# Where the narrow products of the next group's x stand in layer 1 of a four-layer kernel

## The chip, the core and the metric

The kernel runs on one core of one Trainium2 chip. The metric is the device time of one execution in microseconds. The engines are named as in the profile: PE is TensorE's matmuls and PEld its weight loads, DVE is VectorE, ACT is ScalarE, POOL is GpSimd and SP is SyncE, which here only issues copies.

## The reference

x has 64 sequences of 32 rows of 512 numbers, so 2048 rows. Four layers follow one another, each of the form x = x + ffn(cond(x)). The change lies in the second of them, layer 1. Its cond part is a gated network with a low-rank addition chosen for each sequence:

```python
def lora_add(base, inp, A, B):          # A[n]: 16 x inputs, B[n]: outputs x 16, n chosen by the sequence
    t = einsum('bri,bni->bnr', A[ids], inp)
    return base + einsum('bor,bnr->bno', B[ids], t) * 0.5
gate = lora_add(x @ W_gate.T, x, A_gate, B_gate)      # 512 -> 1376
up   = lora_add(x @ W_up.T,   x, A_up,   B_up)        # 512 -> 1376
act  = silu(gate) * up
down = lora_add(act @ W_down.T, act, A_down, B_down)  # 1376 -> 512
```

Its ffn part takes the result through a 512 x 512 product with a bias and a gated mixture of eight low-rank updates; its output is added to x. Layer 0 is a mixture over squared ReLU features, layer 2 attention over a cache of keys and values, and layer 3 again products with low-rank updates. All numbers are float32.

## The kernel before

Layer 1 is `layer1`, from L323. It works on groups of two tiles of 128 rows, so a group is 256 rows, or eight sequences, and there are eight groups. The products of a group are held transposed: features stand on the partitions and the 256 rows in the free dimension.

A product with a sequence's own A is narrow. For two sequences at a time the 16 rows of A for each stand side by side, so that a product has 32 columns of weights and 64 moving columns; four such products, one for each pair of sequences, fill four strips of 32 output partitions in one PSUM tile. `low` (L416) does this for x: two matrices (gate and up), four slices of 128 inputs and four pairs of sequences, 32 products into `low_ps`. `low_down` (L428) does it for the activations: eleven slices of features and four pairs, 44 products into `low_d_ps`. Each is followed by `masked` (L407), one VectorE instruction that multiplies the result with a mask, so that each sequence keeps its own 16 numbers, and writes `low_x` or `low_d`. Those are the inputs of one more full-width product each with the gathered B rows: `features` (L439) uses `low_x` with Bg1 and Bu1, and `down` (L455) uses `low_d` with Bd1.

A product of float32 appears in the profile as two matmuls and two weight loads, so one call of `product` makes two records on PE and two on PEld.

The order of TensorE's work is written out by hand: `on_pe` (L76) makes each matmul follow the one written before it. The loop from L539 goes over the groups. `new` is the group in work, `old` the one before, whose ffn part (`choose`, `base`, `turn`, `out`) is spread between the features of `new`, and `then` the one after. Eleven calls of `features` make the 1376 features (the last has 96). In between, `then` gets its gathered rows and its A copies (`load_updates`, L378), its x (`load_x`), the transposes of it (`x`, L398) and a rearranged copy of A for x (`firsts("x")`, L387, on VectorE, tile `first_x`). At the end stand the down products: `new.down(range(NFC - 1), False)` makes 4 x 10 products over the first ten feature slices into `pz`, and `new.down((NFC - 1,), True)` makes, for each of four output slices, one product for the last feature slice and one with Bd1, and then copies `pz` to `zT`. This place, from the first down product to the first gate product of the next group, is called a turn; the group after it exists in seven of the eight cases.

The other engines' lists are ordered by a scheduler. In the program before, VectorE's list has, behind the last features of a group, the masking of `low_d`, the copy `first_down` for the next group, the masking of `low_x`, the copy `first_x` for the group after that (each group has one place for `first_x`, and the copy waits for eight A copies), and the copy to `zT`. SyncE's queue issues the A copies, x and the blocks of weights for `sum_up` (L274) in a chain; `sum_up` prepares sums of layer 2's weights on GpSimd beside the features, and the gathered Bg1, Bu1 and Bd1 rows are issued on GpSimd behind the last sum.

Of the kernel before, what the change touches and what calls it, by code (L numbers as in the profile page):

```python
# [322 lines left out]
def layer1(c, kp, x_in, x_out, sums):  # L323

    tc, nc, a = c.tc, c.nc, c.a
    G = 2
    N = G * P  # L330
# [5 lines left out]
    with ExitStack() as ctx:  # L336
# [28 lines left out]
        def product(out, lhsT, rhs, start, stop):  # L365
            c.on_pe(nc.tensor.matmul(out, lhsT, rhs, start=start, stop=stop))  # L366

        class Group:
# [70 lines left out]
            def features(self, f):  # L439

                if f == 0:
                    self.actT = gp.tile([P, NFC, N], F32, name="actT")
                o, w = FC[f]
                acc = ps.tile([P, 2, N], F32, tag="acc", bufs=4, name="gate_up")
                for u, (wt, n) in enumerate(((wg, "Bg1"), (wu, "Bu1"))):
                    for k in range(KC):
                        product(acc[:w, u, :], wt[:, k, o:o + w], self.xT[:, k, :],
                                u == 0 and k == 0, False)
                    product(acc[:w, u, :], self.B[n][:, o:o + w], self.low_x[:, u, :], False, u == 1)
                sg = tp.tile([P, N], F32, name="sg")  # L450
                nc.scalar.activation(sg[:w], acc[:w, 0, :], AF.Sigmoid)  # L451
                nc.vector.tensor_tensor(sg[:w], sg[:w], acc[:w, 0, :], ALU.mult)  # L452
                nc.vector.tensor_tensor(self.actT[:w, f, :], sg[:w], acc[:w, 1, :], ALU.mult)
# [85 lines left out]
        for g, new in enumerate(groups):  # L539
            old = groups[g - 1] if g else None  # L540
            then = groups[g + 1] if g + 1 < len(groups) else None
            parts = [f for _ in range(5) for f in next(to_sum)]

            def features(f):
                new.features(f)
                if f < len(parts):
                    parts[f]()

            features(0)
            if old:  # L550
                old.choose(0)
            features(1)
            if old:
                old.choose(1)
            features(2)
            new.firsts("down")
            if then:
                then.load_updates()
            features(3)
            if old:  # L560
                old.turn(0)
                old.base(0)
                old.out(0)
            features(4)
            if old:
                old.turn(1)
                old.base(1)
                old.out(1)
            if then:
                then.load_x()  # L570
            features(5)
            features(6)
            features(7)
            if then:
                then.x(0)
            features(8)
            if then:
                then.x(1)
            features(9)
            if then:  # L580
                then.firsts("x")
            features(10)
            new.down(range(NFC - 1), False)
            new.low_down()
            if then:
                then.low()
            new.down((NFC - 1,), True)
        for f in (new.choose, new.base, new.turn, new.out):
            for t in range(G):
# [897 lines left out]
def emit(tc, a, layers=(0, 1, 2)):  # L1487
    with ExitStack() as ctx:
# [11 lines left out]
        for n in layers:  # L1500
            out = rows("out") if n == layers[-1] else scratch(f"x{n}")
            if n == 0:
                layer0(c, x, out)
            if n != 0 and n == next(m for m in layers if m):
                kp = ctx.enter_context(tc.tile_pool(name="known", bufs=1))
                last = Tail(c)
                last.numbers(kp)
                known = Known(c, kp)
                sums = {}
                for h in range(HALVES):  # L1510
                    sums["in", h] = dram.tile([P, GB, 4, KC // 2, D], F32, name=f"in_sums{h}")
                    sums["out", h] = dram.tile([P, HQP // 2, 4, D // 2], F32, name=f"out_sums{h}")
            if n == 1:
                layer1(c, kp, x, out, sums)
            elif n == 2:
                y_part, y = scratch("y_part"), scratch("y")
                attention(c, known, x, y_part, y, sums, last.between(x, y, out))
            x = out
# [86 lines left out]
```

## Time and profile before

| what | us |
|---|---|
| median of 3 plain runs | 3589.3 |
| lowest and highest | 3585.83, 3597.19 |
| the profiled execution, whole | 3603.64 |
| its span, first to last instruction | 3601.9 |
| TensorE matmul busy (98% of the span) | 3526.7 |
| TensorE weight loads busy (73%) | 2634.1 |
| VectorE busy (60%) | 2154.5 |
| GpSimd busy (44%) | 1598.8 |
| layer 1, about | 388 to 1073 |

Where the text speaks of a moment it is counted from the start of the span. A line of the chain of waits, or of the timeline, has the start, the duration, and then what ran: engine, line, output and inputs by the program's names, and how many of them. "issue" is time in which an engine waited for nothing that the profile shows. The granted clock is the share of TensorE's full clock that it was given.

### The profile page before, as it was taken

How to read it: one execution, taken by the hardware profiler on the slowest of the kernel's cores; microseconds unless marked ns; L12 is line 12 of the kernel's file. 1: busy time of each engine (PE TensorE's matmuls, PEld its weight loads, DVE VectorE, ACT ScalarE, POOL GpSimd, SP SyncE). 2: the span in 40 equal slices, each digit the busy share in tenths (PEclk: the TensorE clock that was granted, in tenths of full speed). 3: DMA queues.
4: the chain of work that ended last, by engine and by line, in shares of the span. 5: the costliest groups of instructions: out<-in, count | busy, mean ns of one | idle time of the engine just before them, and what ended most of it. 6: DMA issues, size and time to landing. Idle time of an engine off the chain costs nothing.

```text
span 3601.9 us, 61460 instructions
## 1 busy us (share of the span) xinstructions
PE 3526.7 (98%) x19328; PEld 2634.1 (73%) x19328; DVE 2154.5 (60%) x5268; ACT 1301.2 (36%) x3110; POOL 1598.8 (44%) x1607
## 2 busy tenths in 40 slices
PE   8999999999998999999999999999999999999999
PEld 3444788877875777787787777877877778777755
DVE  5443222222227777778778677787787777877433
ACT  1111111111113545444454454444544544444311
POOL 0112332222207546456455464564564655644232
PEclk9999999999999999999999999999999999999999
DMA  5003543333226777888877878788878788877731
GB/s 210 27 26 136 174 135 125 103 103 105 101 72 213 249 243 249 256 248 257 255 248 253 258 247 255 249 257 258 255 254 263 245 264 253 256 253 223 217 94 63
DMA packets 610340, 715.99 MB, mean 199 GB/s; under 512 B 61826, under 2 KB 469378, under 8 KB 610018
## 3 DMA queue, kind: packets, MB, share of 16 engines
q1 hardware_dynamic: 557538, 539.01, 48.2%
q0 software_dynamic: 50176, 168.86, 13.4%
q10 hardware_dynamic: 2304, 4.20, 0.3%
q8 instruction: 157, 2.57, 0.3%
q14 instruction: 165, 1.35, 0.1%
HBM read 669.88 MB, written 41.94 MB: 198 GB/s over the span
## 4 chain that ended last, share of the span: by engine, by line
PE 84%; DVE 8%; DMA 3%; issue 2%; POOL 1%; ACT 1%; SPq 1%; DVEq 0%; another core or an unknown queue 0%; ACTq 0%; POOLq 0%
PE po L712 12%; PE gate_up L366 11%; PE py L712 11%; PE sc L993 10%; PE pq L712 7%; PE prT_ps L707 5%; PE pkv L712 5%; PE pz L366 5%; PE po L1371 3%; PE ph L126 3%; PE pd L251 3%; PE po L366 2%; PE qkT_ps L707 1%; PE py L206 1%; DVE pr L1005 1%
## 5 line engine op out<-in xcount | busy, mean ns | idle before, releaser
L738 POOL DMA_INDIRECT vt<-in_v_rows,v_rows x512 | 510.9, 998 | 313.3 <-PE po L712 189.8
L1000 ACT ACTIVATE pr<-pr,low 128x544 f32<-128x544 f32 x512 | 383.3, 749 | 688.1 <-DVE low L998 556.3
L993 PE MATMUL sc<-kt,qT 128*128 128x288 f32 (+1 forms) x2048 | 557.2, 395 | 15.5 <-DVE low L998 12.6
L993 PEld LDWEIGHTS sc<-kt,qT 128*128 128x128 f32 x2048 | 386.2, 191 | 232.2 <-issue 129.3
L712 PE MATMUL po<-prT,vt 128*128 128x128 f32 x4096 | 546.9, 277 | 4.8 <-ACT prT L1011 3.1
L712 PEld LDWEIGHTS po<-prT,vt 128*128 128x128 f32 x4096 | 522.3, 192 | 39.6 <-ACT prT L1011 20.7
L998 DVE CUSTOM_DVE_ANT_0 pr<-sc,mask 128x544 f32<-128x544 f32 x512 | 368.4, 719 | 142.9 <-PE sc L993 119.2
L786 POOL TENSOR_TENSOR projected<-projected,swapped 128x512 f32<-128x512 f32 x160 | 208.3, 1302 | 313.5 <-DVE projected L785 284.5
L1005 DVE TENSOR_SCALAR pr<-pr,low 128x512 f32<-128x512 f32 x512 | 318.4, 622 | 12.6
L1011 ACT COPY prT<-prT_ps 128x512 f32<-128x512 f32 x512 | 294.0, 574 | 75.3 <-PE sc L993 30.8
L707 PE MATMUL prT_ps<-ident,pr 128*128 128x128 f32 x2048 | 312.5, 275 | 1.8 <-DVE pr L1005 1.7
L707 PEld LDWEIGHTS prT_ps<-ident,pr 128*128 128x128 f32 x2048 | 238.5, 142 | 10.4 <-issue 2.1
L712 PE MATMUL py<-wo,oT 128*128 128x256 f32 x1024 | 241.8, 379 | 0.0
L712 PE MATMUL pq<-wp,x_sums 128*128 128x512 f32 x512 | 240.2, 593 | 0.0
L1002 DVE RECIPROCAL low<-low 128x1 f32<-128x1 f32 x512 | 82.1, 160 | 229.7 <-ACT pr L1000 195.3
L712 PEld LDWEIGHTS py<-wo,oT 128*128 128x128 f32 x1024 | 186.5, 190 | 21.1
L1003 ACT ACTIVATE own_pr<-pr,low 128x32 f32<-128x32 f32 x512 | 164.8, 322 | 93.6 <-DVE low L1002 68.5
L452 DVE TENSOR_TENSOR sg<-sg,gate_up 128x256 f32<-128x256 f32 (+1 forms) x88 | 37.0, 421 | 269.3 <-ACT sg L451 265.9
L130 POOL TENSOR_TENSOR rs<-rs,minus_half 128x4 f32<-128x4 f32 x160 | 180.6, 1129 | 23.3 <-DVE low L1002 15.7
L712 PE MATMUL py<-wo,o_sum 128*128 128x256 f32 x768 | 182.9, 382 | 2.3 <-DVE o_sum L929 2.3
L712 PE MATMUL pq<-wp,xT 128*128 128x512 f32 x384 | 182.2, 597 | 0.2 <-issue 0.2
L745 DVE COPY own_vt<-v 32x128 f32<-32x128 f32 x512 | 164.1, 320 | 22.8 <-issue 4.0
(242 smaller groups left out, 5856.2 us busy)
## 6 DMA issues: line engine op xcount, KB each, us to landing
kt<-in_kT SPq DMA_DIRECT2D x2048, 64.0 KB
wp<-in_sums SPq DMA_DIRECT2D x192, 512.0 KB
wo<-out_sums SPq DMA_DIRECT2D x128, 512.0 KB
wp<-in_WqT SPq DMA_DIRECT2D x96, 512.0 KB
wo<-in_WoT SPq DMA_DIRECT2D x96, 512.0 KB
wp<-in_WkT SPq DMA_DIRECT2D x32, 512.0 KB
xt<-x SPq DMA_DIRECT2D x48, 256.0 KB
in_sums<-sums POOLq DMA_DIRECT2D x24, 512.0 KB, 5.1
```

The costliest lines, as they stand in the source:

```text
L130: self.nc.gpsimd.tensor_tensor(t, t, self.minus_half[:, :n], ALU.pow)
L366: c.on_pe(nc.tensor.matmul(out, lhsT, rhs, start=start, stop=stop))
L707: c.on_pe(nc.tensor.transpose(pt[:, m, :], piece, c.ident))
L712: c.on_pe(nc.tensor.matmul(out, lhsT, rhs, start=first and i == 0, stop=last and i == len(pairs) - 1))
L738: nc.gpsimd.indirect_dma_start(out=vts[b % 2][:, n, :], out_offset=None, in_=a["v_rows"], in_offset=bass.IndirectOffsetOnAxis(ap=rows[h][: ...
L786: nc.gpsimd.tensor_tensor(src, src, tmp, ALU.add)
L993: c.on_pe(nc.tensor.matmul(sc[:, lo + n * PSIZE:lo + m * PSIZE].rearrange("p (n k) -> p n k", k=PSIZE), q, kt[:, n:m, g, :], start=True, s ...
L998: nc.vector.tensor_tensor_reduce(pr[:, :NK], sc[:, lo:lo + NK], masks[h, b], -SCALE, 3.0e38, ALU.add, ALU.min, low[:, 0:1])
L1000: nc.scalar.activation(pr[:, :NK], pr[:, :NK], AF.Exp, bias=low[:, 0:1], scale=-1.0, accum_out=low[:, 1:2])
L1003: nc.scalar.activation(own_prs[b % 2][:, g * S:(g + 1) * S], pr[:, L:NK], AF.Copy, scale=low[:, 2:3])
L1005: nc.vector.tensor_scalar(pr[:, :L], pr[:, :L], low[:, 2:3], None, ALU.mult)
L1011: last_prT.append(nc.scalar.copy(prT, pt).ins)
```

## The change

In each turn with a group after it, `then.low()` moves from behind `new.low_down()` to ahead of the first down products. Nothing is added or left out. In the built program, VectorE's list changes with it: the masking of `low_x` and the copy `first_x` for the group after next come ahead of the masking of `low_d` and the copy `first_down`. The lists of ScalarE, GpSimd and SyncE are the same as before.

```diff
             features(10)
+            if then:
+                then.low()
             new.down(range(NFC - 1), False)
             new.low_down()
-            if then:
-                then.low()
             new.down((NFC - 1,), True)
```

## The prediction

> **What bounds the kernel now.** I read the page first: TensorE is busy 3526.7 us of the 3601.9 us span, so time is saved only where TensorE itself stands still or runs slowly. The queue list of the same page holds a second fact that matters here: a queue of kind "instruction", q8.
>
> ```profile
> PE 3526.7 (98%) x19328; PEld 2634.1 (73%) x19328; DVE 2154.5 (60%) x5268; ACT 1301.2 (36%) x3110; POOL 1598.8 (44%) x1607
> ...
> q8 instruction: 157, 2.57, 0.3%
> ```
>
> 2.57 MB in 157 packets is 16.4 KB each. TensorE has 2 x 19328 = 38,656 records (a weight load and a matmul count one each), and 38,656 / 157 = 246 records a packet. I take q8 to be TensorE's own code.
>
> Next, the chain of waits, cut to layer 1. The change acts at a place that comes seven times, where a group has a group after it; I number these turns 1 to 7 and measure each from the first down product to the first gate product of the next group. Turns 6 and 7:
>
> ```profile
> 867.34 17.27 PE pz L366 x80
> 884.61 1.37 PE low_d_ps L366 x88
> 885.97 0.89 PE low_ps L366 x62
> 886.86 4.07 issue
> 890.93 0.42 PE low_ps L366 x2
> 891.35 6.28 PE pz L366 x16
> ...
> 956.67 17.27 PE pz L366 x80
> 973.94 1.37 PE low_d_ps L366 x88
> 975.31 0.89 PE low_ps L366 x64
> 976.20 3.66 PE pz L366 x16
> ```
>
> Turn 7 is the clean one: 17.27 + 1.37 + 0.89 + 3.66 = 23.2 us. In turn 6 TensorE stops for 4.07 us two records before the end of the narrow products, with no semaphore to blame ("issue"), and then needs 6.28 us instead of 3.66 for the same 16 products. The stretches of all seven turns, with busy times by engine (PE, PEld, DVE, ACT, POOL), then granted clock, DMA share and GB/s:
>
> ```profile
> 442.32:467.69 25.37, 24.23 (x250) 20.73 (x249) 4.07 (x6) 0.97 (x2) 14.24 (x19) 1.00 0.64 206
> 526.74:550.99 24.25, 23.35 (x249) 20.31 (x249) 3.98 (x6) 0.97 (x2) 8.94 (x12) 1.00 0.51 168
> 610.03:633.23 23.20, 23.20 (x250) 20.32 (x249) 3.98 (x6) 0.97 (x2) 8.73 (x12) 1.00 0.49 165
> 692.27:719.50 27.23, 25.03 (x250) 21.50 (x249) 3.98 (x6) 0.97 (x2) 9.20 (x12) 0.94 0.46 150
> 778.55:808.29 29.74, 26.43 (x249) 22.44 (x249) 3.98 (x6) 0.97 (x2) 9.39 (x13) 0.89 0.46 150
> 867.34:897.63 30.29, 26.22 (x249) 22.36 (x249) 4.08 (x6) 0.97 (x2) 8.97 (x12) 0.89 0.43 143
> 956.67:979.87 23.20, 23.20 (x250) 20.32 (x249) 3.38 (x5) 0.97 (x2) 11.02 (x17) 1.00 0.40 138
> ```
>
> Against 23.20 the excess is 2.17, 1.05, 0, 4.03, 6.54, 7.09 and 0: **20.9 us** in all. Turns 2, 4, 5 and 6 hold 0.90 + 2.20 + 3.31 + 4.07 = 10.5 us of "issue" in one piece each; the other 8.2 us of their 18.7 are the slow clock after it (granted clock 0.50 in 715.8 to 719.1, 801.1 to 807.8 and 889.9 to 896.5). Turn 1 stutters in four short pieces.
>
> Why does TensorE stop? The DMA view, cut to turn 6, shows no q8 packet from 884.6 to 888.4, while POOL's queue q0 moves 0.86 MB at a DMA share of 62%; the q8 packet comes at about 888.5, and TensorE goes on at 890.9. In turn 7 the same kind of packet passes in 973.0 to 974.5 with no other traffic, and nothing stops. Over the first three microseconds or so of the narrow products the DMA share was 0.93, 0.73, 0.77 and 0.62 in the four stalled turns, and 0.15 and 0.03 in the clean ones. So I read it thus: 88 + 64 narrow products are 304 records in 2.26 us, more than one packet of code, and the next packet stands behind the gathered Bg and Bu rows that POOL issued a few microseconds earlier (880.71 and 882.03 in turn 6).
>
> **The change part by part.** Nothing is added or taken away. TensorE's order is written out by hand, so its list follows the source: in each turn the 32 products of low (64 records of each kind) go ahead of the 40 down products, and low_down's 44 stand alone behind them. ScalarE's, POOL's and SyncE's lists stay as they are, every DMA with them. On VectorE two instructions go ahead of low_d: the masking of low_x (0.68 us) and the copy of first_x for the group after next (0.68 us).
>
> (1) The code supply. The narrow run of 304 records becomes 128 (0.89 us) and 176 (1.37 us), with 160 wide records, 17.27 us, between. A packet of 246 records that holds all of low_down holds 70 wide records, 35 matmuls at 0.216 us (17.27 / 80): 7.6 + 1.4 = 9.0 us of work. The slowest packet, turn 6, took 6.3 us (884.61 to 890.93), counted from the start of the narrow run. Counted so, it now comes in time with 2.7 us to spare. Value: from 0 (the stall only moves) to +20.9 us. I count turns 2 to 6 in full (18.7 us) and half of turn 1 (1.1 us), whose stutter begins before its packet and has another look: **+19.8 us**.
>
> Here a rule speaks against the gain. The Trainium skill, "Runtime: NRT & Kernel Launch", section "Instruction fetch mechanics", says that crossing a 16 KiB boundary of code is mostly hidden, because instructions are dispatched more slowly than the store of code is refilled. By the rule the 20.9 us aren't code and term (1) is nothing; the change would then cost only term (2), 3590.7 us. The row decides: 304 records in 2.26 us are 7.4 ns each, and the stops end 1.4 us after a q8 packet has run. The page's packet of 256 instructions agrees with the 246 above.
>
> (2) Lost cover for low_d. Before, low's 0.89 us stood between low_down and the products with Bd1, which need VectorE's masked low_d (0.42 us). Now one down product of 0.43 us is all. The trace has this arrangement already, in the last group, which has no group after it:
>
> ```profile
> 1055.23 1.44 PE L366 MATMUL low_d_ps<-actT,first_down 128*32 128x64 f32 x88
> 1056.60 0.70 PE L366 MATMUL pz<-actT,down1T 96*128 96x256 f32 x2
> 1056.73 0.42 DVE L410 TENSOR_TENSOR low_d<-low_d_ps,own 128x256 f32<-128x256 f32 x1 [17.39 <-PE low_d_ps L366]
> 1057.21 0.70 PE L366 MATMUL pz<-low_d,Bd 128*128 128x256 f32 x2
> ```
>
> There the chain gives 3.86 us to the 16 products instead of 3.66: 0.2 us, times seven: **-1.4 us**. Queued behind the waiting product are the other six products of this tail and the next group's gate products, so all of it is on the path. If VectorE were late, each microsecond would count in full.
>
> (3) low comes earlier. It needs xT: ScalarE's second copy follows the second transpose (517.66 in turn 2), a whole pair of features, 8.63 us, before low would start. It needs first_x, copied a turn earlier, and for the first turn at 425.03, 17 us ahead. Both are hidden, 0; if xT came late the wait would stand in front of the down products one for one.
>
> (4) low_x is ready some 18 us sooner. Its reader, the Bg product at 552.34 in turn 2, found it done (547.30 + 0.68) anyway: 0.
>
> (5) VectorE's queue. The copy of first_x waits for eight A copies, and low_d, the next first_down and the copy of zT now queue behind it. The A copies were issued at 522.95 to 526.63 in turn 2, and the hardware queue's traffic was over by about 532; low_down would end at 526.7 + 0.89 + 17.27 + 1.37 = 546.2, so 14 us are left. Turns 3 to 6 issue A at the same place. Turn 1 is the tight one: A issued until about 455, traffic over by 459.5, low_down over at 461.8. Hidden, 0, with 2.3 us of cover there.
>
> Sum: 19.8 - 1.4 = 18.4 us. The profiled execution took 3603.6 us (1.7 us around the span), so its like would take 3585.2. The median of the plain runs, 3589.3, is 14.3 us lower; the order of the code is the same in both, so I carry the difference over whole: 3589.3 - 18.4 = **3571 us**, -0.5%.
>
> **The rivals.** (a) The plain runs stall less than the profiled one, since the wait for code depends on DMA traffic in that execution. For it: turns 3 and 7 don't stall at all. Against it: four of seven do, and the copies in their way are the kernel's own. With half of the gain, 9.9 - 1.4 = 8.5: 3581 us.
>
> (b) The change doesn't do what it says: TensorE still runs dry, now in the single runs or just behind them, since the same records pass. For it: the 6.3 us may have begun earlier than I count, and 9.0 us isn't far above. Against it: the last group's low_down, alone among wide products, ran with no stop, and turn 2 lost only 0.9 us at the highest DMA share. Then 20.9 is kept and 1.4 lost: 3591 us.
>
> (c) Slower: VectorE's wait for A. If A lands after low_down's end, low_d is held back by the copy of first_x, and TensorE with it. It decides once A lands over 19.5 us after a turn begins; to be slower than before with the stalls gone it takes (18.4 + 10.8) / 7 = 4.2 us more in each turn. Now A lands at about 5 us in turn 2 and 17 us in turn 1. It could come later if POOL's sums, which SyncE's queue waits for ahead of A, fall behind the faster groups. With 5 us in each turn: 3589.3 - 18.4 + 35 = 3606 us.
>
> **How the numbers follow.** A plain comparison of this kernel tells about 0.3% (10.8 us) from no change. Likeliest case 0.70, own range 3564 to 3578; (a) 0.14; (b) 0.10; (c) 0.06. Half of (a) may lie over the bound, as its gain runs from 4 to 13 us: faster 0.70 + 0.09 = 0.79, same 0.05 + 0.10 = 0.15, slower 0.06. The range: up to 3586 it takes in most of (a), down to 3562 a gain of 27 us, some 6 more than the profile shows, for plain runs that stall longer. Left out are (b), (c) and a little more.
>
> **What would show it.** Right: seven turns near 23.4 us from the end of the features to the next gate product (0.89 + 17.27 + 1.37 + 3.86), no "issue" over 0.5 us beside low_ps or low_d_ps, granted clock 1.00 from 400 to 1060. Wrong: idle time of one to four microseconds with a q8 packet in it behind low_d_ps; VectorE's low_d released by an A copy; the Bd product later than 0.3 us behind low_d; or the same stops elsewhere in the layers behind, whose code comes at other moments beside their DMAs.

## The result

The changed kernel took 3575.2 us, the median of six runs (3569.5 to 3582.5), against 3592.8 us for the kernel before in six runs beside them and earlier (3585.8 to 3597.3). The ratio is 0.9963, with a 95% interval of 0.9950 to 0.9977: faster by 0.37%, which is 13 us by the ratio and 17.6 us by the medians. Run twice more, each time beside the kernel before on the same chip, it came to 0.9970 (0.9956 to 0.9984) and 0.9960 (0.9947 to 0.9974). The forecast was 3571 us in a range of 3562 to 3586, so time and direction were right.

These are the seven turns of the changed kernel, each from its first narrow product of x to the first gate product of the next group, with the same columns as the seven rows shown of before (busy time of PE, PEld, DVE, ACT and POOL, then granted clock, DMA share, GB/s):

```profile
443.18:466.89 23.71, 23.71 (x249) 20.48 (x250) 4.48 (x6) 0.97 (x2) 13.84 (x18) 1.00 0.60 193
525.93:549.64 23.71, 23.71 (x250) 20.47 (x250) 4.66 (x6) 0.97 (x2) 9.27 (x12) 1.00 0.49 168
608.69:632.40 23.71, 23.71 (x249) 20.48 (x250) 4.08 (x6) 0.97 (x2) 8.83 (x12) 1.00 0.49 163
691.44:715.15 23.71, 23.71 (x250) 20.48 (x250) 4.08 (x6) 0.97 (x2) 9.18 (x12) 1.00 0.55 169
774.20:797.90 23.70, 23.70 (x249) 20.47 (x250) 4.08 (x6) 0.97 (x2) 10.07 (x13) 1.00 0.61 194
856.95:880.66 23.71, 23.71 (x250) 20.48 (x250) 4.51 (x6) 0.97 (x2) 9.32 (x13) 1.00 0.56 184
939.71:963.42 23.71, 23.71 (x249) 20.48 (x250) 3.38 (x5) 0.97 (x2) 10.12 (x15) 1.00 0.45 152
```

Every turn is the same, PE is busy through each of them, and the clock is full. The sum is 166.0 us; before it was 183.3, so the turns gave 17.3 us. The profiled executions differ by more, 3603.6 - 3582.5 = 21.2 us; the other 3.9 us lie outside the turns. The chain of waits shows what one turn is made of, here turn 6, the one that had stopped for 4.07 us:

```profile
856.95 1.03 PE low_ps L367 x64
857.98 17.46 PE pz L367 x80
875.45 1.37 PE low_d_ps L367 x88
876.82 3.85 PE pz L367 x16
```

No "issue" is left. But low costs 1.03 us where it had cost 0.89, the down products 17.46 instead of 17.27, and the tail 3.85 instead of 3.66: each turn is 0.51 us longer than the clean turn of before (23.20 us). The first two differences, 0.33 us, were not in the forecast.

### The profile page after: what moved, and what is told of

It is laid out like the page before. It is cut to its first block, busy times and chain, and to the rows that moved or that the text cites. A ratio compares the mean times of both kernels' runs of the same rounds, so it can differ in the third digit from the quotient of the medians.

```text
span 3580.7 us, 61453 instructions
## 1 busy us (share of the span) xinstructions
PE 3519.5 (98%) x19328; PEld 2630.8 (73%) x19328; DVE 2156.9 (60%) x5268; ACT 1297.6 (36%) x3110; POOL 1598.2 (45%) x1607
## 3 DMA queue, kind: packets, MB, share of 16 engines
q14 instruction: 165, 1.35, 0.1%
## 4 chain that ended last, share of the span: by engine, by line
PE 88%; DVE 4%; DMA 4%; issue 1%; POOL 1%; ACT 1%; SPq 0%; DVEq 0%; ACTq 0%; POOLq 0%
PE po L713 13%; PE sc L994 11%; PE py L713 11%; PE gate_up L367 11%; PE pq L713 8%; PE prT_ps L708 6%; PE pkv L713 5%; PE pz L367 5%; PE po L1372 3%; PE ph L126 3%; PE pd L251 3%; PE po L367 2%; PE qkT_ps L708 2%; DMA wp<-in_sums 1%; PE py L206 1%
## 5 line engine op out<-in xcount | busy, mean ns | idle before, releaser
L708 PEld LDWEIGHTS prT_ps<-ident,pr 128*128 128x128 f32 x2048 | 238.0, 142 | 10.9 <-issue 2.7
L288 POOL TENSOR_TENSOR sums<-blocks 128x256 f32<-128x256 f32 x40 | 28.9, 723 | 330.6 <-DMA blocks<-in_WoT 109.7
```

Source lines behind the costliest of these rows:

```text
L708: c.on_pe(nc.tensor.transpose(pt[:, m, :], piece, c.ident))
```

## The experiments

The question was what stops TensorE, and why the change ends it. The code theory says that a packet of code comes too late when it is used up in one narrow run while the next waits in the DMA queues. Its main rival was that a long narrow run stops by itself, wherever the packets end; the question beside it was how much POOL's gathers have to do with it.

**Where the stops stand.** The traces answer part of this without an edit. TensorE's list in the kernel before has 40,373 instructions: 38,656 matmuls and weight loads, 1,714 that handle semaphores, and three more. q8 brought 157 packets of 16,384 bytes; at 256 instructions each these are 40,192, so a packet holds 256, and the forecast's 246 had left out the semaphores. Counted in the order in which they ran, these are the instructions ahead of each long stop:

| profile | turns | instructions ahead of the stop |
|---|---|---|
| kernel before | 2, 4, 5, 6 | 4801, 6849, 7873, 8897 |
| kernel before, once more (below) | 2, 3, 4, 5, 6 | 4801, 5825, 6849, 7873, 8897 |
| no gathers (below) | 5, 6, 7 | 7873, 8897, 9921 |

Divided by 256, every one of these twelve leaves 193. So these stops are whole packets apart, as packet ends are, wherever in the turn they fall. The four of turn 1 aren't (211, 221, 100 and 111 are left). In the kernel before, a group takes 1030 instructions, six more than four packets, so the packet end moves six back from one turn to the next: from the tail in turn 2 to the last products of low in turn 6.

**The packet ends moved, the order kept.** Ahead of layer 1's first narrow products:

```diff
+        spare = ps.tile([P, P], F32, tag="lo", bufs=2, name="spare")
+        for n in range(32):
+            product(spare[:, :64], c.ident, c.ident[:, :64], n == 0, n == 31)
         groups[0].low()
```

> The kernel before, with 32 small products of the identity (128x64 moving, two matmuls and two loads each, 128 records) put once ahead of layer 1's first narrow products. Their result is read by nobody. The order of the turns stays: 304 narrow records in one run. Code theory: all later packet ends move by 128 records against the turns. Where TensorE ran dry after 300 to 322 records of the narrow run, packet ends now lie at about 172 to 194, and the packet that begins there holds some 120 narrow, 32 tail and 100 feature records, over 14 us of work, so it is refilled in time: turns 2, 4, 5 and 6 fall to about 23.2 us, excess over all turns under 4 us instead of 20.9, and a plain time 12 to 18 us under the kernel before (the added products cost 2 us). Rival, narrow run as such: 304 narrow records beside POOL's gathers stop TensorE wherever the packets end; excess stays at 15 to 25 us, plain time within 5 us of before.

The ratio to the kernel before was 0.9986 (0.9979 to 0.9992), with a median of 3593.1 against 3596.4 us. Turn 6 in its chain of waits:

```profile
863.54 17.27 PE pz L366 x80
880.80 1.37 PE low_d_ps L366 x88
882.17 0.89 PE low_ps L366 x64
883.07 3.67 PE pz L366 x16
```

TensorE's order is that of before, 304 narrow records in one run, and there is no stop, in this turn or in any other: the sum of these rows is 23.2 us, and the periods from group to group are 82.24 us, all six. Only the place of the packet ends has changed. The rival falls. The plain time gained 3 to 5 us and not 12 to 18, for the most part because the added products cost some 10 us and not 2. They ran at half clock (0.51 granted from 387.8 to 400.55 us), which by itself explains no more than a factor of two:

```profile
387.80 12.75 PE L366 MATMUL spare<-ident 128*128 128x64 f32 x60
```

Layer 1's first narrow product came at 400.5 us instead of 390.2. In the profiles layer 1 still ended 10.9 us sooner than in the first profile of before (1062.2 against 1073.1).

**Half that shift.** The same with `range(16)`, 64 records.

> The kernel before with 16 small products of the identity, 64 records, ahead of layer 1's first narrow products; it runs dry, if at all, 64 records earlier in the narrow run, about 236 to 258 records into it. Two readings of when a packet of code is asked for. If it is asked for when the packet before it begins to run, that is 2 us ahead of the narrow run and behind GpSimd's gathers (issued 2 to 4 us ahead of it): stops in turns 5 and 6 as long as before or 0.5 us longer, 4 to 5 us. If it is asked for some 40 records sooner, because TensorE's queue is filled ahead of its work, that is 6 us ahead of the narrow run and ahead of the gathers: no stop over 0.6 us in turns 4 to 6, group periods of 82.2 to 82.5 us. Rival, narrow run as such: stops of 1 to 4 us as in the kernel before.

One run, 3573.8 us, and again no stop of 0.2 us or more in any turn, with periods of 82.24 us and one of 82.43. So of the two readings the second holds, and the traces bear out its 40 records: in the first profile of before, seven of layer 1's 31 packets began exactly 41 instructions ahead of the end of the packet in work, and none more than 45 ahead. In the kernel before this point falls on the start of the narrow run, behind POOL's gathers; 64 records sooner it falls among the wide products, ahead of them. Turn 6 of this run: q8 from 869.5 to 871.0 us (packets, MB, share), then Bg:

```profile
q8 instruction: 1, 0.02, 3.9%
```

```profile
874.53 1.00 POOL L360 DMA_INDIRECT Bg<-in_Bg,rows  x1 [0.30 <-issue]
```

The packet began at 869.88 us, 4.7 us ahead of Bg's issue. In turns 2, 4 and 5 it was ahead as well, by 0.2 to 1.8 us; in the same four turns of the kernel before it began 6.4 to 7.8 us behind Bg's issue.

**No gathers.**

```diff
-                self.B = {n: gather(n, g) for n in ("Bg1", "Bu1", "Bd1")}
+                self.B = ({n: gather(n, g) for n in ("Bg1", "Bu1", "Bd1")} if g < 2
+                          else groups[g - 2].B)
```

> The kernel before, but groups from the third on use the gathered Bg1, Bu1 and Bd1 rows of the group two before them, so 18 of 24 gathers are left out and the layer computes with the wrong rows there. TensorE's list is unchanged. Code theory with the queue: the packet of code no longer stands behind the gathers. Turns 2, 4, 5 and 6 lose most of their stop and their slow clock, excess under 5 us in all, plain time 12 to 18 us under the kernel before. Rival, the packet is late by itself: the narrow run takes 2.26 us and any packet takes longer, so each of these turns keeps a stop of 1 to 2 us, excess 8 to 15 us. Rival, narrow run as such: unchanged, 15 to 25 us.

The ratio was 0.9971 (0.9960 to 0.9982), 3587.5 against 3596.4 us: 9 us less, somewhat under what was expected. Turns 2 to 4 have no stop; in turns 5, 6 and 7 a small one grows. Turns 6 and 7 in the chain of waits:

```profile
871.58 0.90 PE low_ps L366 x64
872.48 0.41 PE pz L366
872.89 0.64 issue
873.52 3.41 PE pz L366 x15
...
954.62 0.89 PE low_ps L366 x63
955.50 1.43 issue
956.93 0.22 PE low_ps L366
957.15 3.66 PE pz L366 x16
```

Turn 6 has lost most of its stop (0.64 us against 4.07), and no stretch of slow clock follows: the products after it take their usual time (3.41 us for 15, 3.66 for 16). The excess of all turns is 0.38 + 0.79 + 1.64 = 2.8 us by the group periods, against 20.9. So some six sevenths of the loss (five sixths of the 17.4 us of the later profile of before) came from the gathers, for the most part in front of the packet. The rest doesn't need them. In turn 7 the q8 packet ran at 954.3, TensorE went dry at 955.5 and went on at 956.9; here POOL had sent out a block of sums at 953.7, and 0.52 MB of q0 moved from 953.0 to 956.9, so it seems that other copies can play the same part, in a smaller way.

**low moved the other way.**

```diff
             new.low_down()
+            new.down((NFC - 1,), True)
             if then:
                 then.low()
-            new.down((NFC - 1,), True)
```

> The kernel before, with low moved the other way: behind the last down products instead of between low_down and them. The two narrow runs (176 and 128 records) are then apart by 32 wide records, 3.7 us. Code theory: a packet that begins 44 to 66 records into low_down holds 110 to 132 narrow, 32 wide and 92 to 114 narrow records, 5.2 to 5.5 us of work, against 4.8 to 6.0 us from that point to the restart in the kernel before: stops of at most 0.8 us, excess of all turns 2 to 7 us, plain time 11 to 17 us under the kernel before. Rival, what helps is low's place ahead of the down products (early low_x, VectorE's order): no gain or a loss here, as low_x comes latest of all, and the Bg product may wait for it.

The ratio was 0.9985 (0.9979 to 0.9992), 3590.6 against 3596.4 us. The long stops and the slow clock are gone here too, with only 32 wide records between the runs and low_x later than in any other version, so low's early place is not what helps. But five turns have a short stop of another kind, always at the same place (turn 2; turn 1 loses 0.65 us beside the issues of Bg and Bu, in low_down):

```profile
546.79 0.80 PE low_ps L366 x46
547.60 0.04 issue
547.63 0.34 PE low_ps L366 x5
547.97 0.42 issue
548.39 0.43 PE low_ps L366 x11
```

These aren't packet ends. The longer stops stand behind 4791, 5822, 6853, 7884 and 8915 instructions, which leave 183, 190, 197, 204 and 211, and in turns 2 and 4 no packet had run for 4 us before them. What is the same in these turns is POOL: it issues the gather of Bd1 as soon as the products with it are done:

```profile
547.07 0.95 POOL L360 DMA_INDIRECT Bd<-in_Bd,rows  x1 [7.74 <-PE pz L366]
```

Turn 7, without a gather, has no stop, and its group period is 82.75 us where the others have 83.75. To see whether the gather is the cause:

**low last, and no gathers** (both edits above together).

> The kernel with low behind the last down products, and without the gathers of Bg1, Bu1 and Bd1 from the third group on (the layer computes with the wrong rows there, as in the second experiment). With the gathers, five of its turns stopped for some 0.4 us, 104 records into low, while GpSimd issued the gather of Bd1, and took 1.0 us more than the turn without one (group periods of 83.75 against 82.75 us). Theory, a gather being issued holds up TensorE's narrow products: all periods at 82.75 us, no stop in low. Rival, this is the end of a code packet, about 312 records from the start of low_down: the stop stays in each turn.

One run, 3576.2 us. The same turn:

```profile
542.57 1.37 PE low_d_ps L366 x88
543.94 3.85 PE pz L366 x16
547.78 1.03 PE low_ps L366 x64
548.82 4.51 PE gate_up L366 x20
```

All periods are 82.75 or 82.76 us. Without the gather the short stop is gone. By itself that would fit a packet behind a gather too; it is the count above that rules a packet end out. Turn 1 of the kernel before, whose stutter the forecast couldn't explain, has the same pattern: Bg was issued at 459.98 and Bu at 462.11 us, both inside its narrow run of 459.6 to 464.0. In the first profile of the changed kernel all gathers but one fall outside the narrow runs; the one that does overlap, Bg at 461.06 in turn 1, left no mark, so not every gather does it. Why a gather that GpSimd issues holds up TensorE isn't shown.

**A first attempt at something better.** low ahead of the last features, and low_down with ten wide products behind it to cover VectorE:

```diff
                 then.firsts("x")
+                then.low()
             features(10)
-            new.down(range(NFC - 1), False)
+            new.down(range(NFC - 1), False, (0, 1, 2))
             new.low_down()
-            if then:
-                then.low()
+            new.down(range(NFC - 1), False, (3,))
             new.down((NFC - 1,), True)
```

> A version meant to beat the changed kernel: low goes ahead of the last features call, and low_down stands between the third and the fourth output slice of the down products, so that ten wide products (4.3 us) cover VectorE's masking of low_d. Code theory: no stops, as in the changed kernel, since the runs of 128 and 176 stay apart. The lost cover of 0.2 us a turn comes back: 1.4 us under the changed kernel, about 15 to 19 us under the kernel before. Rival: low ahead of the last features meets an xT that isn't copied yet, or the added switch between wide and narrow costs another 0.15 us a turn: equal to the changed kernel or 1 us over it.

The ratio was 0.9981 (0.9973 to 0.9990), 3589.3 us: under the kernel before, but far from what was expected. Two things went wrong, and both are in the profile. In turn 1 VectorE's list shows the wait for A that the forecast had as its slower rival:

```profile
456.47 0.69 DVE L391 COPY first_x<-A 128x1024 f32<-128x1024 f32 x1 [17.62 <-DMA blocks<-in_WqT]
457.08 0.41 DVE L452 TENSOR_TENSOR sg<-sg,gate_up 96x256 f32<-96x256 f32 x1
457.52 0.42 DVE L453 TENSOR_TENSOR actT<-sg,gate_up 96x256 f32<-96x256 f32 x1
```

low stood ahead of the last features, so the copy of first_x stood ahead of the last features' work in VectorE's list, and could only run once a load had landed (the profile names the next copies in SyncE's queue; VectorE had been idle for 17.6 us); low_down then waited 1.35 us for that work. And in turns 4 and 5 low_down ran where Bg and Bu are issued. Turn 4:

```profile
705.30 1.06 PE L366 MATMUL low_d_ps<-actT,first_down 128*32 128x64 f32 x51
705.51 1.01 POOL L360 DMA_INDIRECT Bg<-in_Bg,rows  x1 [0.30 <-issue]
706.77 0.32 PE L366 MATMUL low_d_ps<-actT,first_down 128*32 128x64 f32 x5 [0.42 <-issue]
706.83 0.99 POOL L360 DMA_INDIRECT Bu<-in_Bu,rows  x1 [0.30 <-issue]
707.51 0.33 PE L366 MATMUL low_d_ps<-actT,first_down 128*32 128x64 f32 x6 [0.42 <-issue]
708.24 0.61 PE L366 MATMUL low_d_ps<-actT,first_down 128*32 128x64 f32 x26 [0.40 <-issue]
```

Three stops of 0.4 us, as in the experiments before, and 2 us more in each of these two turns.

**The kernel before, once more.** No edit.

> The kernel before once more, unchanged, on another chip, for its profile. The profiled execution shown earlier took 3603.6 us, and the plain runs of before beside the first experiments had a median of 3596.4. If the stops depend on which traffic a packet of code meets, as the code theory has it, the turns with stops keep their places in TensorE's list (the packet ends are the same) but not their lengths: excess over all turns between 5 and 21 us. If each stop is fixed by the program, the excess is 20 to 22 us again, turn by turn.

Its ratio to the other runs of the same program was 1.0005 (0.9994 to 1.0016). Its turns took 24.27, 23.49, 23.43, 24.51, 30.34, 30.27 and 23.45 us by the chain of waits, an excess of 17.4 us. Turn 5, from low on:

```profile
792.85 0.90 PE low_ps L366 x64
793.75 0.41 PE pz L366
794.16 3.73 issue
797.89 6.67 PE pz L366 x15
```

The stop stands at the same product as in the first profile (there 3.31 us), and turns 5 and 6 are the long ones again, while turns 2 and 4 shrank from 1.05 and 4.03 us of excess to 0.29 and 1.31. The places are the program's, the lengths are the execution's.

**The changed kernel, once more.** No edit, beside the last one, and again in a later set.

> The changed kernel once more, unchanged, beside the experiments and on their chip. Code theory: no stop in any turn, each 23.7 us as in its first profile, and a plain time 10 to 18 us under the kernel before. If the first gain came partly from the later layers by chance, the gain is 5 to 10 us here, with the same turns.

> The changed kernel unchanged, beside that version on the same chip: 0.30 to 0.45% under the kernel before, no stop in any turn, group periods of 82.75 us.

The ratios were 0.9970 (0.9956 to 0.9984; 3584.2 against 3593.0 us) and 0.9960 (0.9947 to 0.9974; 3575.3 against 3587.6 us). All group periods are 82.75 or 82.76 us but one of 83.01: in turn 6 of the first, low_down paused for some 0.25 us, at no packet end but beside the issue of Bu at 874.47. There is no longer stop in either.

**The changed kernel with its packet ends moved** (the 32 products of the first experiment).

> The changed kernel with the 128 records of small identity products ahead of layer 1's first narrow products, as in the first experiment. These cost some 8 to 10 us at the start of layer 1, where the clock is slow, as they did there. Code theory: with the runs of 128 and 176 records apart, no place of the packet ends makes TensorE run dry, so every turn stays at 23.7 us. If the changed kernel only has a lucky place of its packet ends, stops of 1 to 4 us appear in some turns.

The ratio was 1.0008 (0.9999 to 1.0017), 3595.8 us, and layer 1 began 10 us late, at 401.3. The turns are untouched: all six periods 82.75 or 82.76 us. So the changed kernel doesn't owe its even turns to a lucky place of the packet ends: they hold with both places that were tried, where the kernel before has its stops with one and not with the other. That the shift made the whole slower by 11.6 us against the changed kernel on the same chip is what the added products cost and a little more.

**A second attempt.** On top of the change:

```diff
-            new.down(range(NFC - 1), False)
+            new.down(range(NFC - 1), False, (0, 1))
             new.low_down()
+            new.down(range(NFC - 1), False, (2, 3))
             new.down((NFC - 1,), True)
```

> A second version meant to beat the changed kernel: as that one, but low_down stands between the second and the third output slice of the down products, 9.6 us behind the start of a turn. There GpSimd issues no gather (they come some 16 us behind it), VectorE's copy of first_x, which in the earlier attempt stood ahead of the last features' work, stays behind it, and 20 wide products cover the masking of low_d. Expected: no stops, turns of 23.5 us instead of 23.7, a plain time 1 to 2 us under the changed kernel. If a gather or an A copy falls on it again, one or two turns get 0.6 to 2 us longer and it equals the changed kernel.

> The version with low_down between the second and the third output slice once more, to see whether its time holds. Its turns were 0.18 us shorter than the changed kernel's, 1.3 us in all, but its plain time was 9.5 us less; most of that lay in layer 2, at stretches of half clock that its profile didn't have. If these come by chance, it is 0 to 4 us under the changed kernel now, if they go with the kernel, 7 to 12 us.

The ratios to the kernel before were 0.9948 (0.9931 to 0.9964; 3574.7 us) and 0.9955 (0.9942 to 0.9968; 3571.1 us), beside 0.9970 and 0.9960 for the changed kernel: 9.5 and 4.2 us less by the medians, with intervals that overlap. Turn 6 of the second run, in the chain of waits:

```profile
853.96 1.03 PE low_ps L367 x64
854.99 8.83 PE pz L367 x40
863.82 1.37 PE low_d_ps L367 x88
865.19 12.30 PE pz L367 x56
```

The sum is 23.53 us against 23.71, as expected; over seven turns that is 1.3 us, and no gather falls on low_down. The rest of what its profiles gained lies where this edit changes nothing: some 2 us ahead of layer 1, and most of it in layer 2. There some 4 us came near the start in both of its profiles. Of the stretch of 1225 to 1240 us, the last profile of the changed kernel comes first, and that of the second run of this one next,

```profile
1225.00:1240.00 15.00, 12.99 (x65) 9.90 (x66) 11.50 (x26) 7.69 (x19) 8.60 (x9) 0.89 0.81 259
```

```profile
1225.00:1240.00 15.00, 13.61 (x99) 11.48 (x98) 12.07 (x26) 8.05 (x20) 11.82 (x14) 1.00 0.79 257
```

a granted clock of 0.89 against 1.00 (the two are at different places of the program: 65 matmuls against 99). A further 7 us of the first run lay at the end of the execution, from about 3230 us, where profiles of one program differ by more among themselves (the changed kernel's three profiles by 9 us). Whether the clock of layer 2's start goes with this edit isn't settled; it was so in two of two profiles, but also in those of the 64-record shift and of low last without gathers. It is the best version found, and neither run clears the changed kernel beyond its interval.

## Why the prediction was right

**(1) The code supply: right, and shown.** The stops ended in all seven turns, in all three profiles of the changed kernel. That the long ones belong to the packets of code and not to the narrow run is shown by their places, all whole packets apart, and by the shifts, which end them with the order of before; that the gathers are most of what delays a packet is shown by leaving them out. The term was 19.8 us, with half of turn 1; the profile gave the whole 20.9, since turn 1's stutter, which belongs to gathers issued inside the narrow run, went as well. The step had put that stutter down to code, so its going was luck, the more as Bg still overlaps a narrow run there. The step counted the packet from the start of the narrow run without knowing when it is asked for. That came out right: in turn 6 of before, the point 41 instructions ahead of the packet end is at 884.54 us, the narrow run began at 884.61, and TensorE went on at 890.93. From that point to the packet's first instruction TensorE had 2.3 us of work there; in turn 6 of the changed kernel it has 14.6 us (862.1 to 876.7). The 9.0 us of the forecast were for the least favourable place of the packet end, so there was more to spare than its 2.7 us.

The rule on the other side, that a boundary of code is mostly hidden (the Trainium skill, "Runtime: NRT & Kernel Launch", section "Instruction fetch mechanics"), holds for the rest of layer 1: in the changed kernel four packets pass in each group, among wide products, with nothing to be seen. It fails where a packet is used up in some 2 us.

**(2) Lost cover for low_d: right.** The tail took 3.85 us against the 3.86 that was read from the last group, 0.2 us a turn, 1.4 us in all. The second attempt at a better version gets it back.

**A term was missing.** One narrow run became two, and each has an entry and an exit that cost time. The timeline of turn 2 of the changed kernel shows the entry:

```profile
525.34 0.59 PE L367 MATMUL gate_up<-low_x,Bu 128*96 128x256 f32 x2
525.86 0.94 PEld L367 LDWEIGHTS low_ps<-xT,first_x 128*32 128x32 f32 x64 [0.36 <-issue]
525.86 1.10 PE L367 MATMUL low_ps<-xT,first_x 128*32 128x64 f32 x64
```

The first narrow weights are loaded 0.36 us after the weight loads before them ended, with no load ahead of its time as among wide products. By the chain, one more entry and exit cost 1.03 - 0.89 and 17.46 - 17.27, 0.33 us a turn and 2.3 us in all. So the loss is 3.6 us, not 1.4, and the sum is 20.9 - 3.6 = 17.3 us instead of 18.4: two errors of size, 1.1 us too little gain and 2.3 us too little loss, that cancel in part.

**(3), (4), (5): right.** None of the waits appeared; VectorE's low_d had been reached in time in every turn. The tight cover of turn 1 in (5) was real: the first attempt at a better version lost 1.35 us to it.

**From the profile to the plain runs.** I carried the difference over whole, 3589.3 - 18.4. The later profile of before had 17.4 us of excess instead of 20.9, which leaves 17.4 - 3.6 = 13.8 us for the change; the three ratios of the changed kernel stand for 13, 11 and 14 us. So the forecast gain of 18.4 us was 4 to 7 us too large for the plain runs, and rival (a), that other executions stall less, holds in part: the lengths vary, the two longest turns hardly. Rival (b) is ruled out by the profiles. Rival (c) did not occur in the changed kernel.

## What to carry to other kernels

Idle time on TensorE that the profile puts down to nothing ("issue"), beside a run of very short products, is worth holding against the times of its code packets: where some 256 instructions run in 2 us, as here, a packet that waits behind copies stops the engine, and the slow clock behind a stop of over 2 us can cost as much again. Keep such runs well under a packet (here 128 and 176 of 256), or put wide products between them; with the two places of the packet ends tried here, the turns then took the same time. To tell such a stop from others, count the instructions ahead of each: those that differ by whole packets are packet ends. Each extra run has its price, here 0.33 us for entry and exit, and it is best placed where GpSimd issues no gathers.

## What the runs showed that wasn't expected

A gather that GpSimd issues can stop narrow products beside it: 0.42 us, five times of five, at the same product, and not once when the gather was left out. The slow clock followed stops of 2.20 us and longer in these turns; after those of 1.43 us and shorter no product was slow. Why isn't shown. Sixty-four records of extra work at the start of layer 1 ended some 17 to 21 us of stops later on. And the small matmuls of the identity, 64 columns wide, took 0.21 us each at half clock (60 in 12.75 us), where the narrow products behind them, at half clock too, took 0.03 us each (64 in 1.94 us).
